# Weights that stay in SBUF and weights that are loaded ahead: the borders between three stages of a graph-network kernel

## The chip, the cores and the metric

The kernel runs on one core of a Trainium2 chip. The core has a matrix engine (PE, with its weight loads shown as PEld), a vector engine (DVE), an activation engine (ACT), a general engine (POOL) and a queue engine (SP) that only issues transfers. ACT and POOL issue transfers too. The metric is the device time of one execution in microseconds (us), median over runs.

## What is computed

Two layers work on 12500 nodes with 256 features each. The first is a weighted sum over 200000 edges followed by a dense layer. The second normalizes the rows, scores four experts for each node by graph attention over 131072 edges and a self-loop each, picks two of the four, and adds their gated outputs.

```python
z = layernorm(x)
x = x + (segment_sum(z[src] * edge_weight[:, None], dst) @ W.T + b)
y = layernorm(x)                                   # 12500 x 256; the experts' input
h = (y @ W_gat).reshape(M, HEADS, NUM_EXPERTS)     # 4 heads x 4 experts
e = leaky_relu((h * att_src).sum(-1)[src2] + (h * att_dst).sum(-1)[dst2], 0.2)
alpha = softmax of e over the edges of each dst2
scores = layernorm(segment_sum(h[src2] * alpha, dst2) + b_gat, ln_gamma, ln_beta).mean over heads
g = softmax over the two highest scores, 0 for the other two experts
x = x + sum over experts of g[:, e] * (gelu(y @ W1[e] + b1[e]) @ W2[e] + b2[e])
```

## The kernel before

Nodes are padded to 98 tiles of 128 rows and worked on in 25 groups of up to four tiles. The program has five stages.

**Head** (to about 150 us). The edge lists are loaded and turned, `x` is normalized and stored as `z_rows`, and the dense layer's `W` is loaded, turned on PE and stored to DRAM as `w_turned` (L246 to L253). A zeroed buffer is stored to `gat_starts` (L254).

**Edge stage** (150 to 2691 us). For each group of edges POOL gathers rows of `z_rows` (L544), PE sums them into windows (L558) and DVE adds the windows to `acc_x`, the sums of all nodes, which lie in SBUF (pool `wide`, 99 x 256 floats, 101 KB of each partition). Beside it the second layer's edges are sorted. The order of PE, DVE and ACT is written out by hand. The stage ends in a branch (L608) on a value, which every engine passes by itself. Its body reads and writes the edge lists and `acc_x` in case an edge group spans more nodes than a window.

**Node stage** (2691 to 2916 us; lines 651 to 773). It loads the turned weights `w_t` from `w_turned`, and `b_all`, `wg` and `att`, by five transfers on ACT's queue (L664 to L668). Then a loop runs over the 25 groups with a lag between its parts: load `x` and add `b_all` on POOL (L690, L701), turn `acc_x` on PE (L680, copied to SBUF by ACT, L681), multiply by `w_t` (L719), add (L721, DVE), normalize, turn back into `yt` (two buffers), store `yt` as `y_t` (L740), multiply by `wg` (L747), form the attention terms in `nds`, store them as `gat_nodes` (L759, ACT's queue) and scatter starts of segments into `gat_starts` (L761, POOL, 98 scatters indexed by `seg2`).

**Expert stage** (2916 to 4590 us; lines 778 to 996). First `starts` is loaded from `gat_starts` (L788), and DVE makes four scans over it and a reduction of `far` (L836 to L860); these temporaries lie in the pool `pre`, which is released after them. Then 100 steps run, one for each group and expert: `up` (L936, two halves, gelu by ACT at L942) and `down` (L960, added by DVE at L964, stored to `expert_rows` at L968). Each group first loads `yt5` from `y_t` (L930). PE's order is written out by hand. Beside it POOL gathers `gat_nodes` by edge (L803), 11 gathers per step and at most four steps ahead of the experts, and DVE runs the attention over blocks of 128 gathers (L874 to L893). The experts' weights `w_1` and `w_2` (16 KB of each partition, each), and the biases `b_in` and `b_2`, are loaded at L912 to L917, after `pre` is released. A short serial piece closes the attention (pool `tail`, L1000 to L1043).

**Mixing stage** (4590 us to the end). Gates are formed for ranges of tiles from rows gathered by POOL (L1076), and the experts' rows are loaded, weighted, summed and stored group by group (L1145 to L1162).

All buffers come from pools that are laid on one another like a stack, lowest address first. A pool waits, by default, when it lands on bytes of released pools: all of its tiles wait for every user of those pools. The transfers, DVE, ACT and POOL instructions outside hand-written regions are put in order by a planner that simulates the program: an engine takes, of what is ready, what stands first in the program. Once placed, an engine's queue is strictly in order.

In the expert stage the stack is, from the bottom: `order` (4 KB), `G` (98.4 KB), `starts` (20.5 KB), then `pre` (`far`, `keep2`, `scan` of 4 KB each, and small ones). After `pre` is released, `w_1`, `w_2`, `b_in` and `b_2` lie on its bytes, and above them `yt5` (two buffers of 4 KB), `fo` and `hh`.

## Time and profile before

| | us |
|---|---|
| median of three runs (lowest, highest) | 4203.77 (4192.69, 4206.19) |
| the profiled execution: its own time | 4920.08 |
| its span, first to last instruction | 4918.3 |
| busy in the span: PE, DVE, ACT, POOL | 3782.7, 2395.4, 1394.8, 2858.2 |

The profiled execution is 17% longer than the median of the runs without a profile; no view says where the extra lies. Times in views are microseconds from the start of the span. A timeline row has a start, a length (several instructions are merged when "x" is over 1), the engine ("SPq" is SP's queue issuing a transfer), the line, the operation, output and input, and in brackets the idle time before it with what ended it. A windows row has the stretch, its length, each engine's busy time with its count of instructions, the granted clock of PE (1.00 is full), the busy share of the 16 transfer engines, and what they moved in GB/s.

### The profile page before, as it was taken

How to read it: one execution, taken by the hardware profiler on the slowest of the kernel's cores; microseconds unless marked ns; L12 is line 12 of the kernel's file. 1: busy time of each engine (PE TensorE's matmuls, PEld its weight loads, DVE VectorE, ACT ScalarE, POOL GpSimd, SP SyncE). 2: the span in 40 equal slices, each digit the busy share in tenths (PEclk: the TensorE clock that was granted, in tenths of full speed). 3: DMA queues.
4: the chain of work that ended last, by engine and by line, in shares of the span. 5: the costliest groups of instructions: out<-in, count | busy, mean ns of one | idle time of the engine just before them, and what ended most of it. 6: DMA issues, size and time to landing. Idle time of an engine off the chain costs nothing. (4 is left out here: it accounts for less than half of the span.)

```text
span 4918.3 us, 54552 instructions
## 1 busy us (share of the span) xinstructions
PE 3782.7 (77%) x18969; PEld 2708.4 (55%) x18970; DVE 2395.4 (49%) x5474; ACT 1394.8 (28%) x3289; POOL 2858.2 (58%) x2825
## 2 busy tenths in 40 slices
PE   0556788878887878878888968889898988889445
PEld 0445566655665656656665855555555555555324
DVE  6555566666666666666665970211202202112267
ACT  4112344433333434333443211112112111112112
POOL 1567566655556556656665776666666666663430
PEclk6778899988998989999998978999999999999667
DMA  7232223322222223222222552222222222221488
GB/s 249 83 86 84 77 84 86 90 78 75 80 79 83 78 78 87 81 78 82 85 84 82 182 159 77 55 52 64 55 47 56 63 51 55 51 60 58 140 211 314
DMA packets 265845, 457.42 MB, mean 93 GB/s; under 512 B 67943, under 2 KB 168705, under 8 KB 264289
## 3 DMA queue, kind: packets, MB, share of 16 engines
q0 software_dynamic: 114128, 219.11, 18.4%
q1 hardware_dynamic: 111663, 207.52, 12.0%
q10 hardware_dynamic: 39778, 27.28, 1.7%
q8 instruction: 153, 2.51, 0.2%
q14 instruction: 123, 1.01, 0.1%
HBM read 334.05 MB, written 119.66 MB: 92 GB/s over the span
## 5 line engine op out<-in xcount | busy, mean ns | idle before, releaser
L544 POOL DMA_INDIRECT gt<-z_rows,src x1563 | 1564.1, 1001 | 1083.3 <-PE win L558 430.1
L803 POOL DMA_INDIRECT G<-gat_nodes,order x1024 | 1021.6, 998 | 549.3 <-issue 287.3
L960 PE MATMUL po<-w,hh 128*128 128x256 f32 x3136 | 749.6, 388 | 137.1 <-issue 92.9
L558 PE MATMUL win<-gt,oh_w 128*128 128x256 f32 x3126 | 811.2, 414 | 27.0 <-DMA gt<-z_rows,src 24.0
L936 PE MATMUL ph<-yt,w 128*128 128x512 f32 (+1 forms) x1600 | 756.1, 613 | 51.1 <-issue 45.2
L960 PEld LDWEIGHTS po<-w,hh 128*128 128x128 f32 x3136 | 607.0, 194 | 325.8 <-issue 194.2
L964 DVE TENSOR_TENSOR fo<-po,b 128x512 f32<-128x512 f32 x196 | 133.9, 689 | 1290.8 <-PE po L960 459.2
L484 DVE TENSOR_SCALAR st<-along,place_l,code 128x1024 bf16<-128x1024 f16 x1024 | 541.7, 570 | 437.6 <-PE place L453 107.4
L558 PEld LDWEIGHTS win<-gt,oh_w 128*128 128x128 f32 x3126 | 639.9, 210 | 128.7 <-issue 26.4
L942 ACT ACTIVATE hh<-ph,b 128x512 f32<-128x512 f32 (+1 forms) x400 | 248.5, 675 | 1255.6 <-PE ph L936 601.6
L550 ACT ACTIVATE oh_w<-hit_w,w 128x128 f32<-128x128 bf16 x1563 | 496.1, 391 | 379.7 <-DVE hit_w L334 165.1
L492 PE MATMUL perm<-st,to_p 128*128 128x512 bf16 x2048 | 568.2, 403 | 0.0
L936 PEld LDWEIGHTS ph<-yt,w 128*128 128x128 f32 x1600 | 319.8, 200 | 381.8 <-issue 364.1
L444 PE MATMUL look<-oh_lo,same_hi 128*128 128x128 bf16 x1024 | 236.1, 231 | 290.3 <-ACT next L456 151.9
L448 PE MATMUL look<-next,oht 98*128 98x128 f32 x2044 | 419.4, 314 | 0.0
L456 ACT ACTIVATE next<-place 98x256 f32<-98x256 f32 x511 | 193.4, 379 | 597.0 <-PE place L453 195.1
L448 PEld LDWEIGHTS look<-next,oht 98*128 98x128 f32 x2044 | 330.7, 204 | 35.9 <-issue 1.6
L463 DVE TENSOR_TENSOR sel<-look,oh_lo 128x512 f32<-128x512 f32 x256 | 175.6, 686 | 327.1 <-remote 119.2
L444 PEld LDWEIGHTS <-same_hi 128*128 128x128 bf16 x1024 | 104.0, 102 | 345.8 <-ACT next L456 191.8
L492 PEld LDWEIGHTS <-to_p 128*128 128x128 bf16 x2048 | 188.4, 102 | 137.9 <-issue 27.4
L436 ACT ACTIVATE same_hi<-bank 128x512 bf16<-128x512 f32 x256 | 152.4, 595 | 377.1 <-PE win L558 94.3
L565 DVE SCALAR_TENSOR_TENSOR acc_x<-win,in,acc_x 128x256 f32 x522 | 247.2, 474 | 19.6 <-PE win L558 15.6
(278 smaller groups left out, 3735.6 us busy)
## 6 DMA issues: line engine op xcount, KB each, us to landing
expert_rows<-fo SPq DMA_DIRECT2D x48, 1024.0 KB
fo_in<-expert_rows SPq DMA_DIRECT2D x24, 2048.0 KB
gt<-z_rows,src POOLq DMA_INDIRECT x1563
G<-gat_nodes,order POOLq DMA_INDIRECT x1024
xt<-in_x SPq DMA_DIRECT2D x24, 512.0 KB
z_rows<-xt ACTq DMA_DIRECT2D x24, 512.0 KB
x_two<-in_x SPq DMA_DIRECT2D x12, 1024.0 KB
x_rows<-x_two SPq DMA_DIRECT2D x12, 1024.0 KB
```

The lines of the kernel that those rows point to most:

```text
L444: first = nc.tensor.matmul(look[:, i % GT + k, :], b["m"][:, i + k, :], one(b["ol"], i + k), start=True, stop=False)
L448: nc.tensor.matmul(look[:, i % GT + k, :], b["oht"][:, i + k, :], nxt[:, k, :], start=False, stop=True)
L484: last = nc.vector.tensor_scalar(st[:, k, :], along, b["l"][:, i + k:i + k + 1], code2[:, c:c + 1], ALU.is_equal, ALU.mult)
L492: first = nc.tensor.matmul(perm[:, h, :], one(b["p"], i + k), st[:, k, h * 512:(h + 1) * 512], start=(c == 0), stop=(c == NC2 - 1), skip_g ...
L544: there = [nc.gpsimd.indirect_dma_start(out=rows[j], out_offset=None, in_=Z, in_offset=IND(ap=idx[:, c:c + 1], axis=0)) for j, c in enumer ...
L550: there += [nc.scalar.activation(hots[j], one(hit, j), AF.Copy, scale=w[:, c:c + 1]) for j, c in enumerate(chunks)]
L558: i = nc.tensor.matmul(win, h, r, start=(j == 0), stop=(j == len(rows) - 1))
L565: return nc.vector.scalar_tensor_tensor(to, win, m, to, ALU.mult, ALU.add)
L803: i = nc.gpsimd.indirect_dma_start(out=G[:, t + 1, :], out_offset=None, in_=NODE, in_offset=IND(ap=order[:, t:t + 1], axis=0))
L936: i = nc.tensor.matmul(ph[:, :n], w_1[:, e, k, f * P:(f + 1) * P], yts[g][:, :n, k, :], start=(k == 0), stop=(k == 1))
L942: i = nc.scalar.activation(item["hh"][:, f, :n * P], ph[:, :n].rearrange("p t m -> p (t m)"), AF.Gelu, bias=b_1[:, e * NF + f:e * NF + f + 1])
L960: m = nc.tensor.matmul(po[:, a, :], item["hh"][:, f, i * P:(i + 1) * P], w_2[:, e, f, :], start=(f == 0), stop=(f == NF - 1))
```

## The change

The turned `W` is no longer stored to DRAM and read back: ACT writes it to `w_t` in a new pool `ahead_of`, which is opened between `first_two` and `wide` and holds `w_t`, `b_all`, `wg` and `att` (3.3 KB) until the end of the node stage. The last three are loaded in the head. The experts' weights get a pool at the very bottom of the expert stage's stack, on the bytes of `first_two`, `ahead_of` and the lower part of `acc_x`, and their loads stand first in that stage's program. `order`, `G` and `starts` lie above them, and `pre` and the experts' `io` pool now begin at the same address, one after the other. All pools of the node and expert stages but `tail` get `reuse_waits="tile"`: each tile waits only for the users of earlier tiles on its own bytes (in PSUM, its own bank).

```diff
-    WT = nc.dram_tensor("w_turned", (D, D), F32).ap()
...
+    ahead_of = tc.alloc_tile_pool(name="ahead_of", bufs=1)
+    w_t = ahead_of.tile([P, 2, D], F32, name="w_t")
+    b_all = ahead_of.tile([P, D], F32, name="b_all")
+    wg = ahead_of.tile([P, 2, HC], F32, name="wg")
+    att = ahead_of.tile([P, 2, HC], F32, name="att")
     wide = tc.alloc_tile_pool(name="wide", bufs=1)
...
         w_in = late.tile([P, 2, D], F32, name="w_in")
         nc.sync.dma_start(w_in, W.rearrange("(c p) i -> p c i", p=P))
-        w_out = late.tile([P, 2, D], F32, name="w_out")
         for i in range(2):
...
-            nc.scalar.activation(w_out[:, i, :], pt[:, :2, :].rearrange("p o q -> p (o q)"), AF.Copy)
-        nc.sync.dma_start(WT.rearrange("(c p) o -> p c o", p=P), w_out)
+            nc.scalar.activation(w_t[:, i, :], pt[:, :2, :].rearrange("p o q -> p (o q)"), AF.Copy)
+        nc.scalar.dma_start(b_all, b[None, :].to_broadcast([P, D]))
+        nc.scalar.dma_start(wg, W_gat.rearrange("(c p) k -> p c k", p=P))
+        for k, a in enumerate((att_src, att_dst)):
+            nc.scalar.dma_start(att[:, k, :],
+                                a.rearrange("h c -> (h c)")[None, :].to_broadcast([P, HC]))
...
-        gp = s2.enter_context(tc.tile_pool(name="gp", bufs=3))
+        gp = s2.enter_context(tc.tile_pool(name="gp", bufs=3, reuse_waits="tile"))
...
+        fixed = s2.enter_context(tc.tile_pool(name="fixed", bufs=1, reuse_waits="tile"))
-        w_t = fixed.tile([P, 2, D], F32, name="w_t")
-        b_all = fixed.tile([P, D], F32, name="b_all")
-        wg = fixed.tile([P, 2, HC], F32, name="wg")
-        att = fixed.tile([P, 2, HC], F32, name="att")
...
-        nc.scalar.dma_start(w_t, WT.rearrange("(c p) o -> p c o", p=P))
-        nc.scalar.dma_start(b_all, b[None, :].to_broadcast([P, D]))
-        nc.scalar.dma_start(wg, W_gat.rearrange("(c p) k -> p c k", p=P))
-        for k, a in enumerate((att_src, att_dst)):
-            nc.scalar.dma_start(att[:, k, :],
-                                a.rearrange("h c -> (h c)")[None, :].to_broadcast([P, HC]))
...
     wide.release()
+    ahead_of.release()
     first_two.release()
     with ExitStack() as s3:
-        big = s3.enter_context(tc.tile_pool(name="big", bufs=1))
-        ps = s3.enter_context(tc.tile_pool(name="ps3", bufs=2, space=PSUM))
+        NF = FF // P
+        wp = s3.enter_context(tc.tile_pool(name="wp5", bufs=1, reuse_waits="tile"))
+        w_1 = wp.tile([P, C, 2, FF], F32, name="w_1")
+        w_2 = wp.tile([P, C, NF, D], F32, name="w_2")
+        b_in = wp.tile([C * NF, P], F32, name="b_in")
+        nc.sync.dma_start(b_in, b1.rearrange("e (f p) -> (e f) p", p=P))
+        for e in range(C):
+            nc.sync.dma_start(w_1[:, e], W1[e].rearrange("(k p) f -> p k f", p=P))
+            nc.sync.dma_start(w_2[:, e], W2[e].rearrange("(k p) d -> p k d", p=P))
+        b_2 = wp.tile([P, C, D], F32, name="b_2")
+        nc.sync.dma_start(b_2, b2[None, :, :].to_broadcast([P, C, D]))
+        big = s3.enter_context(tc.tile_pool(name="big", bufs=1, reuse_waits="tile"))
+        ps = s3.enter_context(tc.tile_pool(name="ps3", bufs=2, space=PSUM, reuse_waits="tile"))
...
-        pre = tc.alloc_tile_pool(name="pre", bufs=1)
+        pre = tc.alloc_tile_pool(name="pre", bufs=1, reuse_waits="tile")
...
         with ExitStack() as s5:
-            wp = s5.enter_context(tc.tile_pool(name="wp5", bufs=1))
-            io = s5.enter_context(tc.tile_pool(name="io", bufs=2))
...
-            w_1 = wp.tile([P, C, 2, FF], F32, name="w_1")
-            w_2 = wp.tile([P, C, NF, D], F32, name="w_2")
-            b_in = wp.tile([C * NF, P], F32, name="b_in")
-            nc.sync.dma_start(b_in, b1.rearrange("e (f p) -> (e f) p", p=P))
...
+            io = s5.enter_context(tc.tile_pool(name="io", bufs=2, reuse_waits="tile"))
+            hp = s5.enter_context(tc.tile_pool(name="hp", bufs=2, reuse_waits="tile"))
+            pe = s5.enter_context(tc.tile_pool(name="ps5", bufs=3, space=PSUM, reuse_waits="tile"))
             b_1 = wp.tile([P, C * NF], F32, name="b_1")
```

More of the change, by code (lines that the diff above doesn't have):

```diff
@@ L651, in gnn_gat_moe @@
     with ExitStack() as s2:
-        gp = s2.enter_context(tc.tile_pool(name="gp", bufs=3))
-        small = s2.enter_context(tc.tile_pool(name="small2", bufs=3))
-        ps = s2.enter_context(tc.tile_pool(name="ps2", bufs=2, space=PSUM))
+        gp = s2.enter_context(tc.tile_pool(name="gp", bufs=3, reuse_waits="tile"))
+        small = s2.enter_context(tc.tile_pool(name="small2", bufs=3, reuse_waits="tile"))
+        ps = s2.enter_context(tc.tile_pool(name="ps2", bufs=2, space=PSUM,
+                                              reuse_waits="tile"))
         flow = [{} for _ in range(NG)]
-        fixed = s2.enter_context(tc.tile_pool(name="fixed", bufs=1))
-        w_t = fixed.tile([P, 2, D], F32, name="w_t")
-        b_all = fixed.tile([P, D], F32, name="b_all")
-        wg = fixed.tile([P, 2, HC], F32, name="wg")
-        att = fixed.tile([P, 2, HC], F32, name="att")
+        fixed = s2.enter_context(tc.tile_pool(name="fixed", bufs=1, reuse_waits="tile"))
         ND = 6
@@ L902, in gnn_gat_moe @@
         with ExitStack() as s5:
-            wp = s5.enter_context(tc.tile_pool(name="wp5", bufs=1))
-            io = s5.enter_context(tc.tile_pool(name="io", bufs=2))
-            hp = s5.enter_context(tc.tile_pool(name="hp", bufs=2))
-            pe = s5.enter_context(tc.tile_pool(name="ps5", bufs=3, space=PSUM))
-            NF = FF // P
-            w_1 = wp.tile([P, C, 2, FF], F32, name="w_1")
-            w_2 = wp.tile([P, C, NF, D], F32, name="w_2")
-            b_in = wp.tile([C * NF, P], F32, name="b_in")
-            nc.sync.dma_start(b_in, b1.rearrange("e (f p) -> (e f) p", p=P))
-            for e in range(C):
-                nc.sync.dma_start(w_1[:, e], W1[e].rearrange("(k p) f -> p k f", p=P))
-                nc.sync.dma_start(w_2[:, e], W2[e].rearrange("(k p) d -> p k d", p=P))
-            b_2 = wp.tile([P, C, D], F32, name="b_2")
-            nc.sync.dma_start(b_2, b2[None, :, :].to_broadcast([P, C, D]))
+            io = s5.enter_context(tc.tile_pool(name="io", bufs=2, reuse_waits="tile"))
+            hp = s5.enter_context(tc.tile_pool(name="hp", bufs=2, reuse_waits="tile"))
+            pe = s5.enter_context(tc.tile_pool(name="ps5", bufs=3, space=PSUM, reuse_waits="tile"))
             b_1 = wp.tile([P, C * NF], F32, name="b_1")
```

## The prediction

> **What bounds the kernel now.** I read the page's slices first (PE is busy 8 to 9 tenths nearly everywhere), then windows by stage, then the queues' waits and the timelines at the two borders that the change touches. The chain of waits covers only the mixing stage and says nothing of these borders. Inside the expert stage PE sets the pace: 91.44 of the 100 us from 3200 are matmuls. Between the node stage and the experts PE has almost nothing:
>
> ```profile
> 2895.00:2900.00 5.00, 4.49 (x32) 3.58 (x31) 4.86 (x25) 1.84 (x5) 3.21 (x4) 0.94 1.11 229
> 2900.00:2905.00 5.00, 4.34 (x21) 3.94 (x20) 1.52 (x7) 0.60 (x1) 3.78 (x5) 0.50 0.74 191
> 2905.00:2910.00 5.00, 1.89 (x8) 1.78 (x8) 0.93 (x6) 0.60 (x1) 1.99 (x3) 0.50 0.22 61
> ...
> 2910.00:2958.00 48.00, 1.57 (x5) 0.60 (x5) 27.27 (x42) 0.00 (x0) 38.40 (x29) 0.50 0.32 100
> ...
> 3200.00:3300.00 100.00, 91.44 (x302) 58.58 (x301) 8.89 (x13) 15.06 (x24) 64.56 (x70) 0.97 0.23 54
> ```
>
> The reader is to see 48 us without matmuls of weight, and transfer engines that are full (share 1.11) until 2900. What ends the hole is in SP's waits and timeline:
>
> ```profile
> SPq L912 <- DVE starts L860: 34.8, 1, 34.8
> ...
> 2917.26 0.32 SPq L788 DMA_DIRECT2D starts<-gat_starts  x1
> 2917.69 0.84 SPq L930 DMA_DIRECT2D yt<-y_t  x2
> 2953.46 0.33 SPq L912 DMA_DIRECT2D b_in<-in_L_ffn_b  x1
> 2953.84 0.42 SPq L914 DMA_DIRECT2D w<-in_L_ffn_W  x1
> ...
> 2926.97 1.07 DVE L836 TENSOR_SCALAR keep<-starts 128x1024 f32<-128x1024 f32 x1 [8.79 <-DMA starts<-gat_starts]
> ...
> 2932.66 1.19 DVE L841 TENSOR_REDUCE spot<-far 128x1 f32<-128x1024 f32 x1
> ...
> 2944.24 9.08 DVE L860 TENSOR_TENSOR_SCAN starts<-keep,c,starts 128x1024 f32<-128x1024 f32 x4
> ...
> 2958.43 13.45 PE L936 MATMUL ph<-yt,w 128*128 128x512 f32 x24 [2.95 <-DMA w<-in_L_ffn_W]
> ```
>
> The weights lie on the bytes of `pre`, so SP holds them for 34.8 us, until DVE's last scan ends at 2953.3. `yt5` was asked for at 2917.69, being above them. The other border and the end of the experts:
>
> ```profile
> 2692.12 0.46 ACTq L664 DMA_DIRECT2D w_t<-w_turned  x1
> ...
> 2695.75 1.57 ACT L681 ACTIVATE agt<-pt 128x512 f32<-128x512 f32 x3 [11.02 <-issue]
> ...
> 2699.87 2.35 POOL L701 TENSOR_TENSOR x_two<-x_two,b_all 128x1024 f32<-128x1024 f32 x1 [28.40 <-DMA x_two<-in_x]
> ...
> 2702.25 0.69 DVE L721 TENSOR_TENSOR x_two<-x_two,po 128x512 f32<-128x512 f32 x1 [9.95 <-POOL x_two L701]
> ...
> 4590.68 0.36 SPq L968 DMA_DIRECT2D expert_rows<-fo  x1
> ...
> 4590.75 0.48 DVE L820 COPY as_rows<-pt 4x128 f32<-4x128 f32 x2
> ```
>
> **The change part by part.**
>
> *Head.* ACT gets four transfers more (0.59 + 0.56 + 0.83 + 0.50 = 2.48 us in the node stage's rows) and SP loses one (0.37). They come after ACT's copy that ends at 132.6; ACT's next instruction is at 150.0, after 17.40 us of waiting for DVE. That cover hides them; without it they cost 2.5. I take 0.
>
> *Border of edge and node stage.* Five issues leave ACT's queue (2692.12 to 2695.18), which held the copies of `agt` until 2695.75, and PE's wait of 3.67 us for `w_t` goes. But the next late thing is already there: DVE's first addition waits for POOL, and POOL for the 1 MB of `x_two`, asked for at 2692.14. The first `x_two` lies on the edge lists, which the branch's body uses, so its tile still waits until DVE has left the branch (2691.5): at most 0.6 us earlier. The `w_t`, `b_all` and small loads (about 0.4 MB) no longer share the engines; at the 263 GB/s of 2710 to 2720 that is 1.5 us. Bounds 0.6 to 3 us, taken 1.5. DVE is busy 194.91 of the stage's 220 us, so its start moves its end.
>
> *Where the experts' weights can start.* By sizes, the new stack is `w_1` (16 KB) on `first_two` (6 KB), `ahead_of` (3.3 KB) and the first 7 KB of `acc_x`; `w_2`, `b_in` and `b_2` on `acc_x` alone. `acc_x` is last read by turns at about 2891; `seg2`, in `first_two`, is read by the last scatter (2914.89), which is also what `starts` waits for. So `w_2`, `b_in` and `b_2` (2.6 MB) are asked for at about 2892, and `w_1` (2.1 MB) at 2917.3, ahead of `starts` since it stands first in the program.
>
> *Early part.* Issuing costs SP 0.33 + 4 x 0.47 + up to 2.60 = 4.8 us; SP's queue is free from 2892.34 (end of the issue at 2891.85) to 2897.03, so that is covered to within a fraction. The bytes are not: they stand before the store of the third last `yt`, issued at 2897.49, for whose buffer ACT waits 6.75 us (until 2907.41), and behind ACT the last `wg` products, `nds`, the last two scatters and `starts`. 2.6 MB at 330 GB/s (2965 to 2970, when weights were loading) are 8 us. If only that store releases ACT, the node stage ends 8 later; if something else does, 0. I take 5, above the middle because the share there is 1.11.
>
> Here a rule of the Trainium skill speaks against the change: "DMA: Bandwidth & Descriptors", "Issuing engines are not separate DMA queues", says that transfers from all issuers run on the same 16 engines and interleave. Its section on the anatomy of a transfer has a fit of 2.0 us plus bytes over 436 GB/s. By the fit `starts` (2.6 MB) takes 8.0 us; the trace has 9.7 (2917.26 to 2926.97). By the fit 2.1 MB ahead of it add 4.8 us; by the trace's 354 GB/s (2960 to 2965) 5.9. I use the trace; by the fit this part would be 1.1 us better and the early part (6.0 in place of 8) about 1.2, so the sum some 2 us better.
>
> *The new wait.* `pre` and `io` now begin at the same address. The first `yt5` buffer lies on `far`, the second on `keep2`. So the load of the first group's `yt5`, which cost nothing before, waits on SP for L841 on DVE, and the second's for L860. What stands behind them on SP is stores of `fo`, not needed until a step is done; who waits for the first is PE. The time: scatters end 2917.3 + 5 = 2922.3; `starts` arrives 9.7 + 5.9 later, 2937.9; L841 ends 6.9 after that (2926.97 to 2933.85 in the rows), 2944.8; `yt5` of 0.5 MB takes about 4 (the first `w_1` took 2953.84 to 2958.43), 2948.8. Against 2958.43 that is 9.6 us earlier. Gelu needs `b_1`, copied by DVE at L921; with `b_in` there by 2900 I expect the planner to put it into DVE's wait for `starts`.
>
> *Expert stage.* PE's 100 steps follow its start. POOL begins 5 us later and PE 9.6 earlier. POOL needs 44 gathers until 2985 + 5 and then 11 x 1.25 = 13.75 us a step; 128 for the first attention block are there at 2990 + 8 x 13.75 = 3100. That block began at 3115.1 and would now begin at 3105. Covered, by 5 us; if not, DVE holds PE's additions for the difference.
>
> *Tail.* `tail` still waits by pool. It lay on the weights, whose last user is PE; it now lies on `io`, whose last user is the store issued at 4590.68. DVE's first copy at 4590.75 therefore waits for 0.5 MB to land: 0.4 + about 3.6 (as above, an estimate) = 4 us; bounds 0 and 5. Behind it lie the gather of `row`, the gathers L1076 and the first gates, which is the chain of waits. `bg` to `nodes` (2.4 us of SP) may go earlier, but the gates, not SP, release the mixing.
>
> *Sum:* -1.5 - 9.6 + 4 = -7 us: 4913 for the profiled execution (4920.08). These are waits of fixed length, so I carry them to the median of plain runs unscaled: 4203.77 - 7 = 4197. 0.3% is 12.6 us, about what a measurement of this kernel can tell from no change.
>
> **The rivals.**
>
> *A, as summed:* chance 0.50; 4188 to 4203.
>
> *B, the queue is kinder:* `starts` goes ahead of `w_1` and the early bytes do not delay the node stage. Then L841 ends at 2933.9, PE starts at 2938, 20.4 earlier; with -1.5 and +4 it is -18: 4186. If also `yt5` didn't land on `far`, PE would start when `w_1` lands, 2922, and the time would be 4170. For it: both loads wait for the same scatter, so a tie decides. Against: ties go to the program's order. 0.26.
>
> *C, slower:* all 4.7 MB stand ahead of `starts`, and `b_1` stays behind the four scans of L860 in DVE's queue. `starts` is late by 14, with the node stage's 8 by 22; the scans end at 2975 and the first gelu follows at 2977, where it was at 2966.4. PE has only four banks for `ph`, so it stands: +11, with the tail +4 and the border -1.5 it is +13: 4217. It turns to a loss once `starts` is late by more than 11.6. For it: L921 stands behind L860 in the program. Against: DVE waits 8.79 us for `starts`. 0.15.
>
> *D, nothing there:* the planner's order makes the loads wait as before, or PE is held by something else at the same time; the tail's +4 and -1.5 remain: 4206. 0.09.
>
> **How the numbers follow.** Faster by over 0.3%: B and the lower edge of A, 0.28. Slower by over 0.3%: most of C and what a changed order of DVE in the expert stage may cost, 0.17. Within: 0.55. The range takes in B's main case and C's lighter ones: 4180 to 4216.
>
> **What would show it.** PE's first L936 at about 2947 (2937 by B, over 2958 by C); SP's wait of L930 on DVE L841 in place of L912 on L860; L788 issued after four L914; DVE L836 starting near 2936; ACT's wait for the last `yt` longer than 6.75; no idle time at L719 for `w_t`, but L721 still waiting for POOL; L820 4 us behind the last L964. I am wrong if PE starts before 2930, if `tail` starts at once, or if the steps themselves take another time.

## The result, and the profile after

| | us |
|---|---|
| before, median of 10 runs beside the changed kernel | 4201.92 (4192.69 to 4206.19) |
| after, median of 10 runs | 4215.93 (4209.60 to 4224.52) |
| ratio, with its 95% interval | 1.0035 (1.0027 to 1.0043) |
| the profiled execution after: its own time, its span | 4211.29, 4209.5 |

The changed kernel is slower by 14.0 us (11.3 to 18.1); a gain of 7 had been forecast. Chips differ: the kernel before takes 4200 to 4203 us on three of them ("the 4200 pace" below) and 4916 to 4919 us on two ("the 4900 pace"), where PE's mean granted clock is lower (0.87 to 0.88 instead of 0.94), and the profile on which the prediction rests, at 4920.08 us, has the second pace. So the trace after is set beside a second trace of the kernel before (run `e12_before_same_chip` below, span 4204.5), and every ratio to before is between runs on one chip.

**The hole between node stage and experts.** One window of the changed kernel (columns as in the prediction's first fence):

```profile
2455.00:2502.00 47.00, 0.75 (x2) 0.16 (x2) 15.94 (x27) 1.28 (x1) 37.53 (x33) 0.50 0.55 175
```

The hole is as long as it was. More is transferred in it (share 0.55, where 48 us of before had 0.32), and PE still has nothing. SP's waits and timeline, then DVE and PE, say why:

```profile
SPq L929 <- DVE spot L853: 21.5, 1, 21.5
SPq L929 <- DVE starts L871: 19.1, 1, 19.1
...
SPq L786 <- DMA gat_starts<-nds,seg: 10.1, 2, 8.9
...
2449.70 0.40 SPq L784 DMA_DIRECT2D b_in<-in_L_ffn_b  x1
2460.57 0.38 SPq L786 DMA_DIRECT2D w<-in_L_ffn_W  x1
2461.00 2.20 SPq L787 DMA_DIRECT2D w<-in_L_ffn_W  x1
...
2470.14 0.55 SPq L799 DMA_DIRECT2D starts<-gat_starts  x1
...
2492.69 19.78 SPq L929 DMA_DIRECT2D yt<-y_t  x2
```

```profile
2460.77 0.17 DVE L920 COPY b<-ph 128x16 f32<-128x16 f32 x1
...
2485.83 1.07 DVE L847 TENSOR_SCALAR keep<-starts 128x1024 f32<-128x1024 f32 x1 [24.89 <-DMA starts<-gat_starts]
...
2491.47 1.19 DVE L852 TENSOR_REDUCE spot<-far 128x1 f32<-128x1024 f32 x1
...
2503.04 9.08 DVE L871 TENSOR_TENSOR_SCAN starts<-keep,c,starts 128x1024 f32<-128x1024 f32 x4
...
2501.34 0.37 PE L829 MATMUL pt<-ident,v 128*4 128x128 f32 x1 [12.76 <-DVE fix_i L862]
...
2502.90 12.09 PE L935 MATMUL ph<-yt,w 128*128 128x512 f32 x24
```

SP waits at L786, the first `w_1`, for the last scatter. `w_2` stands behind it, since the loop alternates the two, and all nine transfers (four of `w_1`, four of `w_2`, and `b_2`; 4.7 MB) go ahead of `starts`, which is asked for 11.0 us after the last scatter's end (2459.1) and lands 15.7 us later. The predicted wait of `yt5` for `far` is there (L929 behind DVE's `spot`). But PE does not start right behind that load: in its queue the transposes of the scans' carries (L829) stand ahead of the first L935.

**The border of edge and node stage.** DVE's first addition came 10.9 us after the cast of `order`, its last instruction of the edge stage (L603; L611 in the changed kernel), in the second trace of before, and 8.3 us in the changed kernel (2239.72 to 2247.97). It waits for POOL, as it did:

```profile
2245.60 4.65 POOL L699 TENSOR_TENSOR x_two<-x_two,b_all 128x1024 f32<-128x1024 f32 x2 [14.75 <-DMA x_two<-in_x]
...
2247.97 1.29 DVE L719 TENSOR_TENSOR x_two<-x_two,po 128x512 f32<-128x512 f32 x2 [7.76 <-POOL x_two L699]
```

**The tail.** First the second trace of before, then the changed kernel, from the last addition of the experts on (timelines of DVE, POOL and SP):

```profile
3925.81 0.69 DVE L964 TENSOR_TENSOR fo<-po,b 128x512 f32<-128x512 f32 x1 [5.68 <-PE po L960]
3926.60 0.48 DVE L820 COPY as_rows<-pt 4x128 f32<-4x128 f32 x2
...
3930.38 0.16 DVE L1007 TENSOR_TENSOR m_row<-m,row 128x4 f32<-128x4 f32 x1 [1.59 <-DMA row<-gat_run,fix_i]
...
3927.24 1.04 POOL L1036 DMA_INDIRECT row<-gat_run,fix_i  x1 [96.69 <-DVE carried L827]
...
3937.33 0.97 POOL L1076 DMA_INDIRECT R<-gat_run,end  x1 [2.02 <-DMA gat_run<-fixed,fix_i]
...
3938.18 0.81 SPq L1062 DMA_DIRECT2D nodes<-gat_nodes  x1
```

```profile
3919.67 0.69 DVE L963 TENSOR_TENSOR fo<-po,b 128x512 f32<-128x512 f32 x1 [5.69 <-PE po L959]
3923.31 0.48 DVE L831 COPY as_rows<-pt 4x128 f32<-4x128 f32 x2 [2.94 <-DMA expert_rows<-fo]
...
3934.45 0.16 DVE L1006 TENSOR_TENSOR m_row<-m,row 128x4 f32<-128x4 f32 x1 [8.84 <-DMA row<-gat_run,fix_i]
...
3924.14 0.94 POOL L1035 DMA_INDIRECT row<-gat_run,fix_i  x1 [99.81 <-DMA bg<-in_L_ffn_b_gat]
...
3941.40 0.96 POOL L1075 DMA_INDIRECT R<-gat_run,end  x1 [2.01 <-DMA gat_run<-fixed,fix_i]
...
3922.73 0.81 SPq L1061 DMA_DIRECT2D nodes<-gat_nodes  x1
```

From the last addition to the first gather of `R`, which opens the mixing, it is 11.5 us before and 21.7 us after. DVE's copy waits 2.94 us for the store of `fo`. Then the gather of `row` takes 10.3 us from its start until DVE uses it (3924.14 to 3934.45), where it took 3.1 before (3927.24 to 3930.38): `nodes` (98 x 24 floats in 128 partitions, 1.2 MB in pieces of 96 bytes) is now asked for 1.4 us ahead of it. Before, `nodes` waited for the whole tail.

The stretches in one table, worked out from the timelines (us, from start to start; each column is one profiled execution at the 4200 pace; the experiments are told below):

| stretch | before, e12 | after | e4 | e5 | e6 | e7 | e15 |
|---|---|---|---|---|---|---|---|
| cast of `order` to first addition | 10.9 | 8.3 | 8.0 | 7.9 | 8.0 | 8.1 | 8.8 |
| first addition to first gather of `G` | 213.0 | 211.4 | 214.0 | 208.9 | 213.9 | 215.5 | 218.3 |
| last `wg` product to first `up` | 49.8 | 52.1 | 49.3 | 48.0 | 35.1 | 9.6 | 50.9 |
| first gather to last addition of the experts | 1458.3 | 1460.3 | 1457.9 | 1459.1 | 1456.7 | 1457.8 | 1458.9 |
| from there to first gather of `R` | 11.5 | 21.7 | 15.8 | 13.9 | 15.6 | 16.3 | 11.5 |
| from there to the end | 267.2 | 268.1 | 266.7 | 268.8 | 267.9 | 267.1 | 268.3 |
| ratio of times to before | 1.0001 | 1.0035 | 1.0013 | 1.0013 | 1.0016 | 1.0019 | 1.0014 |

From the cast on, after against before: -2.6 - 1.6 + 2.0 + 10.2 + 0.9 = +8.9 us (the third row overlaps its neighbours and is not in the sum). The edge stage ends at 2239.7 after and 2243.6 before, but in the traces whose edge stage has the same code it ends anywhere from 2237.1 to 2246.2, so a single trace says nothing there. Nor can this pair hold all of the 14.0 us: its two executions took 4211.29 and 4206.27 us, 5.0 apart, the one 4.6 under its kernel's median and the other 3.3 over that of the runs beside it.

### The profile page after: what moved, and what is told of

It reads as the page before. It is cut to its first block, busy times and chain, and to the rows that moved or that the text cites. A ratio compares the mean times of both kernels' runs of the same rounds, so it can differ in the third digit from the quotient of the medians.

```text
span 4209.5 us, 54518 instructions
## 1 busy us (share of the span) xinstructions
PE 3542.2 (84%) x18969; PEld 2600.8 (62%) x18970; DVE 2390.4 (57%) x5474; ACT 1421.5 (34%) x3289; POOL 2902.5 (69%) x2825
## 3 DMA queue, kind: packets, MB, share of 16 engines
q0 software_dynamic: 114128, 219.11, 21.3%
q1 hardware_dynamic: 111391, 207.26, 13.9%
## 5 line engine op out<-in xcount | busy, mean ns | idle before, releaser
L552 POOL DMA_INDIRECT gt<-z_rows,src x1563 | 1603.5, 1026 | 603.3 <-issue 403.0
L566 PE MATMUL win<-gt,oh_w 128*128 128x256 f32 x3126 | 767.4, 397 | 200.2 <-DMA gt<-z_rows,src 150.4
L566 PEld LDWEIGHTS win<-gt,oh_w 128*128 128x128 f32 x3126 | 596.3, 197 | 316.9 <-issue 192.9
L959 PE MATMUL po<-w,hh 128*128 128x256 f32 x3136 | 721.2, 384 | 51.0 <-ACT hh L941 36.4
L959 PEld LDWEIGHTS po<-w,hh 128*128 128x128 f32 x3136 | 603.1, 193 | 219.8 <-issue 87.5
L935 PE MATMUL ph<-yt,w 128*128 128x512 f32 (+1 forms) x1600 | 706.6, 585 | 0.0
L941 ACT ACTIVATE hh<-ph,b 128x512 f32<-128x512 f32 (+1 forms) x400 | 249.5, 676 | 1046.8 <-PE ph L935 1044.4
L500 PE MATMUL perm<-st,to_p 128*128 128x512 bf16 x2048 | 524.1, 378 | 0.0
L935 PEld LDWEIGHTS ph<-yt,w 128*128 128x128 f32 x1600 | 304.6, 190 | 288.9 <-issue 277.5
L456 PE MATMUL look<-next,oht 98*128 98x128 f32 x2044 | 393.8, 300 | 0.0
L456 PEld LDWEIGHTS look<-next,oht 98*128 98x128 f32 x2044 | 309.5, 192 | 37.6
L342 DVE TENSOR_TENSOR oh_hi<-twice,hi 128x784 bf16<-128x784 bf16 x256 | 143.4, 560 | 96.8 <-PE place L366 96.7
```

Of the source, the lines that this page charges most:

```text
L456: nc.tensor.matmul(look[:, i % GT + k, :], b["oht"][:, i + k, :], nxt[:, k, :], start=False, stop=True)
L500: first = nc.tensor.matmul(perm[:, h, :], one(b["p"], i + k), st[:, k, h * 512:(h + 1) * 512], start=(c == 0), stop=(c == NC2 - 1), skip_g ...
L552: there = [nc.gpsimd.indirect_dma_start(out=rows[j], out_offset=None, in_=Z, in_offset=IND(ap=idx[:, c:c + 1], axis=0)) for j, c in enumer ...
L566: i = nc.tensor.matmul(win, h, r, start=(j == 0), stop=(j == len(rows) - 1))
L935: i = nc.tensor.matmul(ph[:, :n], w_1[:, e, k, f * P:(f + 1) * P], yts[g][:, :n, k, :], start=(k == 0), stop=(k == 1))
L941: i = nc.scalar.activation(item["hh"][:, f, :n * P], ph[:, :n].rearrange("p t m -> p (t m)"), AF.Gelu, bias=b_1[:, e * NF + f:e * NF + f + 1])
```

## The experiments

**The kernel before again.** Unchanged code, three times.

> The kernel before, unchanged, for a profile of an execution as long as the runs without one, so that its stages can be set beside those of the changed kernel (span 4209.5). Time: 4203, ratio 1.000. If the loss is made at the border of node stage and experts alone, the stretch from the last `wg` product to the first L936 is about 12 us shorter here than the 52 us of the changed kernel; if it is made in the experts' steps, the stretch is equal and the experts last some 12 us less here than the 1412 us (2502.9 to 3914.6) of the changed one.

> The kernel before, unchanged, once more for a profile on a chip where it takes 4200 us, to set its stages beside those of the changed kernel (first addition of the node stage to last `wg` product 202.8 us; last `wg` to first L935 52.1; first to last gather 1364.0; last gather to last L935 91.2; start of the last addition of experts to `fixed` 18.3; from there to the end 271). Theory 'POOL and the first attention block pace the experts': the pause before the experts is 48.5 us here, 3.6 shorter, but the stretch from first to last gather and the 91 us behind it are the same within 3 us, so the border's 3.6 us are not in the result; the tail is 10 us shorter. What is left of the 14 us must then stand in the node stage or ahead of it. Rival: the gathers' stretch is shorter here, and the loss is made in the experts' steps.

> The kernel before, unchanged, for a trace of an execution of about 4200 us. In five traces of changed kernels at that length the stretches are: first addition of the node stage to first gather 209 to 215 us, first gather to last addition of the experts 1457 to 1460 us, start of that addition to `fixed` 18.3 us (8 with `tail` by tile). With `tail` by tile the changed kernel still measured 1.0013 [1.0007, 1.002] of before, 5.5 us. If the tile waits or the new stack lengthen the node stage, this trace has it 5 us or more shorter (about 205); if they lengthen the experts, their stretch is 5 us or more shorter here (about 1452); if both agree within 2 us, the rest stands ahead of the node stage, in the head or the edge stage.

The first two ran at the 4900 pace: 1.0028 (1.0005 to 1.0052) and 0.9995 (0.9966 to 1.0024). The first is the same kernel and its interval still leaves out 1, so at that pace a ratio tells nothing under half a per cent, and only local stretches are used of those traces. The third gave the column above: the node stage is no shorter in it than after (213.0 against 211.4), the experts' stretch agrees within 2.0 us, the tail is 10.2 shorter. So in this pair neither the tile waits nor the new stack lengthened the two stages; what is left is the tail, and some 5 of the 14 us that no stretch of the pair holds.

**Which wait holds the start of the experts** (e1, then e3; 4900 pace).

```diff
         b_in = wp.tile([C * NF, P], F32, name="b_in")
-        nc.sync.dma_start(b_in, b1.rearrange("e (f p) -> (e f) p", p=P))
-        for e in range(C):
-            nc.sync.dma_start(w_1[:, e], W1[e].rearrange("(k p) f -> p k f", p=P))
-            nc.sync.dma_start(w_2[:, e], W2[e].rearrange("(k p) d -> p k d", p=P))
         b_2 = wp.tile([P, C, D], F32, name="b_2")
-        nc.sync.dma_start(b_2, b2[None, :, :].to_broadcast([P, C, D]))
...
         nc.sync.dma_start(starts, STARTS[:E2, :].rearrange("(p l) c -> p l c", l=L2))
+        nc.sync.dma_start(b_in, b1.rearrange("e (f p) -> (e f) p", p=P))
+        for e in range(C):
+            nc.sync.dma_start(w_1[:, e], W1[e].rearrange("(k p) f -> p k f", p=P))
+            nc.sync.dma_start(w_2[:, e], W2[e].rearrange("(k p) d -> p k d", p=P))
+        nc.sync.dma_start(b_2, b2[None, :, :].to_broadcast([P, C, D]))
```

```diff
         pre = tc.alloc_tile_pool(name="pre", bufs=1, reuse_waits="tile")
+        pad = pre.tile([P, 2 * L2], F32, name="pad")
         far = pre.tile([P, L2], F32, name="far")
```

> The changed kernel with one thing moved: the loads of the experts' weights stand behind the load of `starts` in the program, not ahead of it. In the changed kernel `starts` was asked for at 2470.14, 11.0 us after the last scatter's end at 2459.1, and DVE's scans could begin at 2485.83. Theory 'queue order' (nine loads in front of `starts` hold it back): `starts` is asked for within 1 us of the last scatter and DVE's L847 begins about 10 to 10.5 us after it, so 16 us earlier; PE's first L935 comes 10 to 16 us earlier, and the time is about 4201. Rival 'new stack' (the loss comes from `yt5` on `far` or from the experts' steps): the time stays within 4 us of 4216.

> The changed kernel with 8 KB of unused bytes laid first in `pre`, so that the two `yt5` buffers lie on no temporary of `pre`; the first load of `yt5` then waits for nothing on DVE. In the changed kernel it was asked for at 2492.69 and PE's first L935 came at 2502.90. Prediction's step (PE waits for this load, and for nothing else): PE starts about 10 us or more earlier, time 4205. Rival 'PE's own queue': two transposes of the scans' carries (L829, L841) stand in PE's queue ahead of the first L935, and they wait for DVE's scans, which end at 2502.5; then PE starts at the same time, the gain is under 1 us and the time 4215.

In e1 `starts` is asked for 8.1 us after the last `wg` product, and the hole is 35.2 us, where it is 48.0 to 52.1 in the six traces with the weights ahead of `starts`: the order in SP's queue was worth 13 to 17 us of PE's start. The ratio was 1.0050 (1.0021 to 1.0078), no gain. In e3 the hole is 49.6 us; the ratio 1.0056 (1.0029 to 1.0084). Its `yt5` was asked for at 2935.53, and PE's timeline shows what it waited for:

```profile
2965.41 0.37 PE L830 MATMUL pt<-ident,v 128*4 128x128 f32 x1 [12.83 <-DVE fix_i L863]
2966.60 0.27 PE L842 MATMUL pt<-ident,carried 4*128 4x4 f32 x1 [0.82 <-DVE carried L840]
2966.80 0.37 PE L830 MATMUL pt<-ident,low 128*4 128x128 f32 x1
2966.96 3.62 PE L936 MATMUL ph<-yt,w 128*128 128x512 f32 x4
```

The experts begin at once behind the transposes. PE's own queue ties them to the scans, 17 us after `starts` has landed; `yt5` on `far` costs nothing.

**The tail** (e4, then e5; 4200 pace).

```diff
-        tail = s3.enter_context(tc.tile_pool(name="tail", bufs=1))
+        tail = s3.enter_context(tc.tile_pool(name="tail", bufs=1, reuse_waits="tile"))
```

```diff
         one = s4.enter_context(tc.tile_pool(name="one", bufs=1))
+        pad = one.tile([P, 12 * 1024], F32, name="pad")
```

> The changed kernel with `tail` too waiting by tile. In the kernel before, the stretch from the start of the last L964 to the copy into `fixed` by the last addition of the tail (L1041) is 8.0 us; in the changed kernel it is 18.3 us: 2.9 us of it before DVE's first copy (the wait for the last store of `fo`), and 10.3 instead of 3.1 us for the gather of `row` (L1035), which was issued 1.4 us behind the load of `nodes`. Theory 'tail': without the wait DVE's copy follows at once, the gather of `row` is issued ahead of `nodes`, and the stretch comes back to 8 to 10 us; 8 to 10 us less in the time. Prediction's step (only the landing costs): 3 to 4 us less, since `nodes` is under way anyway. Rival 'elsewhere': the stretch shrinks, and the time does not, since another thing (load of `nodes`, `fo_in`) then holds the mixing stage.

> The changed kernel with 48 KB of unused bytes laid first in pool `one`, so that `one` lands on `G` as well and its loads (`bg` to `nodes`) wait for the end of the tail's work on `G`, as before the change; `tail` still waits by pool for the last store of `fo`. Theory 'nodes in front of row': the gather of `row` takes 3 us again and not 10.3, the first copy still waits 2.9 us, and the tail's stretch is 11 us instead of 18.3; 7 us less in the time. Rival: the gather is slow for another reason (behind the store of `fo`), and the stretch stays at 17 to 18 us.

Both measured 1.0013 (e4 1.0007 to 1.0020, e5 1.0006 to 1.0020), by the ratios some 9 us better than the changed kernel. In e5, with `nodes` held back, the gather of `row` takes 2.4 us (3920.22 to 3922.63), the first copy still waits 2.78, and the tail is 13.9 us: `nodes` was some 7 of the 10.2 us. In e4 the gather slips past `nodes`, but the scatter of `fixed` behind it does not:

```profile
3925.55 1.01 POOL L1042 DMA_INDIRECT gat_run<-fixed,fix_i  x1 [10.04 <-DVE fixed L1040]
3934.81 0.96 POOL L1075 DMA_INDIRECT R<-gat_run,end  x1 [8.25 <-DMA gat_run<-fixed,fix_i]
```

POOL waits 8.25 us for the scatter where it waited 2.02 before. The stretch that the expectation named came back to 6.1 us, but the wait moved to the scatter: to the first gather of `R` e4 gave back 5.9 of the 10.2 us.

**Both repairs, and an early start** (e6, e7; 4200 pace). e6 is e1 with e4's tail. In e7, which has e4's tail too, `w_2` lies on the bytes that the scatters read and `w_1` on `acc_x` alone; the first `yt5` has a place of its own; `far`, `keep2` and `scan` lie in rows of `G`; and the scans with their transposes are a function that is called behind step 3.

```diff
-        w_1 = wp.tile([P, C, 2, FF], F32, name="w_1")
         w_2 = wp.tile([P, C, NF, D], F32, name="w_2")
+        w_1 = wp.tile([P, C, 2, FF], F32, name="w_1")
...
+        yt_0 = wp.tile([P, GT, 2, P], F32, name="yt_0")
+        nc.sync.dma_start(yt_0, YT[:, :GT])
         for e in range(C):
             nc.sync.dma_start(w_1[:, e], W1[e].rearrange("(k p) f -> p k f", p=P))
-            nc.sync.dma_start(w_2[:, e], W2[e].rearrange("(k p) d -> p k d", p=P))
...
         nc.sync.dma_start(starts, STARTS[:E2, :].rearrange("(p l) c -> p l c", l=L2))
+        for e in range(C):
+            nc.sync.dma_start(w_2[:, e], W2[e].rearrange("(k p) d -> p k d", p=P))
...
+        def spare(row):
+            return G[:, row:row + 43, :].rearrange("p l c -> p (l c)")[:, :L2]
...
+        far = spare(800)
...
+                    if step == 3:
+                        scans()
```

> The changed kernel with both repairs: the experts' weights loaded behind `starts`, and `tail` waiting by tile. The stretch from the last `wg` product to the first L935 was 35 us with `starts` first (52 in the changed kernel, 48.5 before). If the two terms add: 17 + 9 us less than the changed kernel, 13 + 3 (start of the node stage) = about 16 less than before where the rest is equal: ratio about 0.996 to before. Rival 'the clock takes it back': the stretches shrink as said, and the first 200 us of the experts get a lower granted clock than after the longer pause (0.89 against 0.92 in the run with `starts` first), so that the time is that of before.

> A version drawn from the readings: `w_2` and not `w_1` lies on the bytes that the scatters still read; `w_1` and the first `yt5` (in a place of its own) are asked for right behind the node stage's last store, then `starts`, then `w_2`; the temporaries of `pre` lie in rows of `G` that are gathered last, so that nothing of the experts lies on them; and the scans' transposes stand in PE's queue behind step 3 and not ahead of the first L935; `tail` waits by tile. If PE's queue and the weights are what holds the experts, PE's first L935 (here L944) comes within 10 us of the last `wg` product, 40 us earlier than in both kernels, and the time is up to 45 us less than before (ratio 0.990). Rival 'POOL is next': POOL's gathers start no earlier and need 13.75 us for 11, a step of PE about 14; PE is held by DVE's attention blocks and gets back 20 us or less.

Ratios 1.0016 (1.0006 to 1.0026) and 1.0019 (1.0012 to 1.0026). PE started 35.1 and 9.6 us after the last `wg` product instead of 52.1, and neither is faster than e4. The row of the table that doesn't move says why: from first gather to last addition it is 1457 to 1460 us in all of them. DVE's waits, of the changed kernel, e6 and e7:

```profile
DVE G L885 <- DMA G<-gat_nodes,order: 128.8, 9, 21.9
```

```profile
DVE G L885 <- DMA G<-gat_nodes,order: 138.9, 9, 24.5
```

```profile
DVE G L893 <- DMA G<-gat_nodes,order: 164.4, 9, 45.7
```

In DVE's queue the first attention block stands behind 16 additions of the experts, eight steps, and needs 128 gathers. They are there 172 to 174 us after the first gather, whenever PE began (2640.1 - 2467.5 before; 2633.5 - 2459.4 after; 171.5 in e7). The additions behind the block wait with it, PE has two banks for `po`, and every later block ties the two again. When PE begins earlier, DVE only comes to the first block earlier and waits longer there: 45.7 us in e7.

PE feels most of this through ACT. ACT's queue is in order too, and the block's exponentials (L894, L896) stand in it ahead of gelus (L941). The second block in the changed kernel:

```profile
2801.74 0.69 DVE L885 TENSOR_TENSOR G<-G,starts 128x512 f32<-128x512 f32 x1 [13.98 <-DMA G<-gat_nodes,order]
...
2807.02 0.63 ACT L894 ACTIVATE starts<-starts 128x512 f32<-128x512 f32 x1 [13.90 <-DVE starts L893]
...
2808.95 1.27 ACT L941 ACTIVATE hh<-ph,b 128x512 f32<-128x512 f32 x2
...
2810.27 5.23 PE L959 MATMUL po<-w,hh 128*128 128x256 f32 x16 [6.04 <-ACT hh L941]
```

Over all of the experts' steps PE waits 36.4 us for ACT and 14.4 us for DVE.

**Is it DVE's order, or POOL's gathers themselves?** First a test of the gathers, at the 4900 pace.

```diff
             for t in range(turn * PER_TURN, min((turn + 1) * PER_TURN, L2)):
+                if t % 16 == 15:
+                    continue
```

> The changed kernel with every 16th of the 1024 gathers of edges left out (their places in `G` are zeroed once by DVE), so the attention of those edges is not computed. Theory 'POOL paces the experts' (a gather takes 0.95 us and 0.30 to the next): 64 gathers less are 64 x 1.33 = 85 us off POOL's 1364; the experts end earlier until PE's own pace holds them (100 steps of about 13.5 us, so at most some 50 us earlier); time 30 to 50 us less than 4216. Theory 'PE paces the experts' (prediction): within 5 us of the changed kernel.

0.9872 of before (0.9833 to 0.9911), 4869.01 against 4919.43: nearer to "POOL paces". But PE's granted clock between 2990 and 4480 us was 0.95, where it is 0.93 in e3, as well, and at this pace POOL sat 247.4 us waiting for the experts' additions. I take it as inconclusive. The order itself:

```diff
-            nc.vector.tensor_add(e, e, d)
+            i = nc.vector.tensor_add(e, e, d)
+            tc.add_manual_dep(i.ins, turned[-1].ins.name, mybir.DependencyInfo(
+                mybir.DependencyClass.Sync, mybir.DependencyReason.DATA),
+                reason="not ahead of its step")
...
-                    if under_way and next(under_way, under_way) is under_way:
-                        under_way = None
+                    for _ in range(1 if step < 90 else 2):
+                        if under_way and next(under_way, under_way) is under_way:
+                            under_way = None
```

This was put on e6 (e10, e13), on e7 (e11, e14), on the kernel before (e16) and on the changed kernel (e17). The first block then stands behind 28 additions (the added dependency keeps a block from going ahead of its step), and in the last ten steps two pieces of a block are taken for one.

> The version with `starts` first and `tail` by tile, and the attention blocks kept from DVE's queue until the step behind which they stand in the program (the first block behind 28 additions of the experts, where it stood behind 16), and two pieces of a block for each of the last ten steps. Theory 'DVE waits in order': in the version without this, DVE sat 139 us in nine waits for gathers with the experts' additions queued behind it, and three versions whose PE began at 2471, 2487 and 2503 all ended the experts 1461 to 1464 us after the first gather. With the blocks later DVE's wait for gathers goes to under 20 us, PE keeps its own pace, and its earlier start counts: experts 20 to 45 us shorter, ratio to before 0.990 to 0.997. Rival 'PE paces': no difference to the version without it (1.0016).

> The version with the experts' early start (first L944 9.6 us behind the last `wg` product) with the same order of the attention blocks. If DVE's wait was what took the early start back, this one is faster than the one before by the 16 us by which PE begins earlier: ratio to before 0.986 to 0.994. If POOL's gathers are the bound whatever DVE does, both are within 5 us of each other.

> The version with `starts` first, `tail` by tile and the attention blocks kept in the program's order, again, where the kernel before takes about 4200 us. It measured 0.9966 [0.9945, 0.9986] where before took 4919 us, while without the order of blocks the same stretch of experts lasted as long whether PE began at 2471, 2487 or 2503. Theory 'DVE waits in order for gathers': DVE's nine waits (139 us) go, PE keeps its own pace (100 steps of 13.5 to 13.8 us), experts 30 to 45 us shorter, ratio 0.990 to 0.994. Rival 'POOL's gathers are the bound whatever DVE does': the last gather comes at the same time, the ratio stays at 1.0016.

> The version with the experts' early start and the blocks in order, again, where before takes about 4200 us (0.9960 [0.993, 0.9989] where it took 4919). By 'DVE waits in order' PE's earlier start by 16 us counts in full: ratio 0.986 to 0.991. By 'POOL is the bound' no faster than the run before this one.

> The kernel before with only the order of the attention blocks changed (the first behind 28 additions of the experts instead of 16, two pieces of a block for each of the last ten steps). In the version with `starts` first and `tail` by tile this took the experts from 1457 to 1381 us behind the first gather where before takes 4200 us (ratio 0.9832). Theory 'DVE waits in order for gathers' holds for the kernel before as well: its nine waits (129 us) go and, as its PE begins 16 us later than in that version, ratio 0.985 to 0.989. Rival 'the new stack is needed': less than half of it.

> The changed kernel as it is (weights ahead of `starts`, `tail` by pool) with the same order of the attention blocks. With DVE no longer waiting for gathers PE's start counts: it comes 52 us behind the last `wg` product, 2 to 3 us later than in the kernel before, and the tail is 10 us longer, so about 12 us more than the kernel before with this order (ratio to it 1.003); against the version with both repairs (0.9832) the 17 us of a later PE and the 10 us of the tail: 0.989 to 0.992 of before. Rival 'the border never counts': only the tail's 10 us more than that version, 0.9855.

At the 4900 pace 0.9966 (0.9945 to 0.9986) for e10 and 0.9960 (0.9930 to 0.9989) for e11: less than the half per cent that a ratio can tell at that pace, and no difference between the two. At the 4200 pace:

| | e16: before | e17: after | e13: both repairs | e14: early start |
|---|---|---|---|---|
| ratio to before | 0.9843 (0.9830 to 0.9857) | 0.9871 (0.9856 to 0.9887) | 0.9832 (0.9819 to 0.9844) | 0.9795 (0.9782 to 0.9808) |
| last `wg` to first `up`, us | 49.1 | 49.3 | 35.6 | 11.3 |
| first `up` to last addition | 1354.1 | 1353.4 | 1352.5 | 1362.4 |
| first gather to last addition | 1394.1 | 1396.0 | 1380.8 | 1365.4 |
| last gather to last addition | 58.1 | 58.1 | 36.4 | 21.3 |
| last addition to first gather of `R` | 11.5 | 21.9 | 15.8 | 16.4 |

DVE's waits for gathers are gone (8.2 us in e14, none in the others), and PE's longest wait within the steps is 2.9 us (e14; 0.8 in the others). The windows of the experts' whole stretch, of before (e12) and of e16:

```profile
2507.90:3925.80 1417.90, 1367.57 (x4737) 908.92 (x4737) 267.38 (x465) 291.62 (x443) 991.95 (x1001) 0.98 0.24 65
```

```profile
2499.56:3853.60 1354.04, 1353.20 (x4737) 902.41 (x4737) 268.41 (x465) 283.60 (x437) 992.13 (x1001) 1.00 0.25 68
```

So it was DVE's order: it cost the kernel before and the changed one alike some 64 us, and it hid every shift of the border. With it gone PE's start counts: the experts end 15 us earlier behind the first gather in e13 than in e17, and 15 more in e14. There two bounds nearly meet: PE is busy for 1355.9 of the 1362.4 us, and the 1024 gathers take 1344 us, with the last addition only 21 us behind the last one. e17 against e16 is 1.0032 (4147.95 over 4134.54), 13.4 us, 10.4 of them in the tail; the border is equal (49.1 and 49.3 us), where I had expected 2 to 3 us. The gain of e13 over e16 was smaller than the 16 us expected: 0.0011, about 5 us, and the two intervals overlap. In the traces 13.3 us are won from first gather to last addition and 2.9 ahead of the first addition; 4.2 are lost in the tail, 2.2 in the mixing and 6.9 in a longer node stage (219.8 against 212.9 us). e14, at 4113.94 us, is some 2% faster than both kernels.

**The head's part alone** (e2 at the 4900 pace, e15 at the 4200 pace): `ahead_of` and its four loads, all else as before.

> The kernel before with the head's part of the change alone: turned W written to `w_t` in `ahead_of`, `b_all`, `wg` and `att` loaded in the head, everything after it as before (pools wait by pool, experts' weights loaded late). Prediction's step: -1.5 us, so 4202 and no difference that can be measured. Rival: the first product of the node stage waits for ACT and SP less than the trace of before let see, up to 5 us gained; or the four loads in the head delay the head's ACT and the edge stage starts later, up to 3 us lost.

> The head's part alone, again, where before takes about 4200 us. Its start of the node stage was 2 us earlier than before's in the traces at 4900 us (8.7 instead of 10.7 and 11.2 us from the cast of `order` to the first addition). If nothing else of the head's part matters: ratio 0.9995. If the 5.5 us that are left with `tail` by tile come from the head or the edge stage (`acc_x` and the edge lists lie 3.3 KB higher): ratio 1.001 to 1.002.

1.0004 (0.9973 to 1.0036) and then 1.0014 (1.0008 to 1.0021): at the 4200 pace it costs 5.9 us (3.4 to 8.8), not 0. The trace has the node stage begin 2.1 us earlier and last 5.3 longer. In the traces the loss lies in a stretch of 15 us that begins 23 us after the cast of `order`; the windows of before (e12) and of e15:

```profile
2266.57:2281.57 15.00, 12.82 (x72) 11.33 (x72) 14.24 (x50) 2.58 (x7) 10.21 (x8) 0.89 0.58 183
```

```profile
2265.43:2280.43 15.00, 12.78 (x59) 11.21 (x59) 12.13 (x39) 2.80 (x6) 8.58 (x6) 0.74 0.53 171
```

In e15 PE's clock falls to 0.50 for some 10 us after a gap of 2.2 us, PE is late, and DVE gets 2.1 us less done. In the changed kernel's trace the same stretch has a clock of 1.00. Of the nine traces at the 4200 pace that have the head's part, four show the dip (0.73 or 0.74; e7, e13, e14, e15), with node stages of 215.5 to 219.8 us, and five don't, with 208.9 to 214.6; the two of before's head and node stage have 0.89 and 213 us. What decides between the two is open. If most executions of the changed kernel had the dip and the profiled one had not, that could be the missing 5 us; this is argued, not shown. Weakly against it: e4 and e5 have the head's part too and measured 5.5 us over before, of which their traces show 4.3 and 2.4 us in the tail, so that 1 to 3 us are left for it.

## Why the prediction was wrong, step by step

Two steps of the sum failed: the new wait, put at -9.6 us, gave nothing, and the tail, put at +4, was 10.2.

*PE's 100 steps follow its start:* this step failed, so that the border's -9.6 us would not have counted even if PE had begun earlier: in e7 it begins 9.6 us after the last `wg` product instead of 52.1, and the experts end only 2.5 us sooner after the first gather. The step was read from "91.44 of the 100 us are matmuls" in a trace at the 4900 pace. Waits of that trace, then of the second trace of before:

```profile
POOL G L803 <- DVE fo L964: 249.0, 55, 11.4
DVE G L874 <- DMA G<-gat_nodes,order: 67.7, 9, 10.6
```

```profile
DVE G L874 <- DMA G<-gat_nodes,order: 129.2, 9, 21.0
POOL G L803 <- DVE fo L964: 30.5, 15, 9.1
```

In the first POOL mostly waits for the experts' additions; at the 4200 pace it is DVE that waits for POOL's gathers. The nine waits of DVE stood in the first trace too, 67.7 us of them, and of these blocks the prediction looked at the first alone: "Covered, by 5 us; if not, DVE holds PE's additions for the difference". The "if not" held.

*Head, 0:* not confirmed. The part alone measured +5.9 us (e15), with its gain at the next border already in it; how much of it is in the changed kernel is open.

*Border of edge and node stage, -1.5 (bounds 0.6 to 3):* right in kind, -2.6 in the pair of traces.

*Where the weights can start, early part +5:* wrong. Only `b_in` went early; `w_2` stood behind `w_1` in SP's queue. I had let `w_2` overtake, against the order of the loop.

*Starts +5.9 late:* its landing took 15.7 instead of 9.6 us, which is the price, but by chance: 4.7 MB stood ahead and not 2.1, and it was asked for 11.0 us after the last scatter, which was not priced. The fit that the prediction sets beside it stands in the Trainium skill ("DMA: Bandwidth & Descriptors", "Anatomy of one DMA — SWDGE (gpsimd) path") for transfers that GpSimd issues, and `starts` goes by SP's queue; the sum rests on the trace, which has 9.7 us.

*New wait on `far`, PE 9.6 us earlier:* the wait is there and decides nothing (e3). Forgotten were the transposes at the head of PE's queue. PE started 2.2 us later in the pair: 48.0 to 52.1 us after the last `wg` product over six traces with the weights ahead of `starts`, against 48.4 to 49.8 in four of the kernel before. So nothing was won of the 9.6.

*Tail, +4 (bounds 0 and 5):* the term that was mis-sized: 10.2 us. The landing was 2.9 of the 4 priced. The other 7 are the loads of `one`: "`bg` to `nodes` (2.4 us of SP) may go earlier, but the gates, not SP, release the mixing". They do go earlier, since `one` now lies on weights that only PE reads, and the small transfers on the gates' path queue behind them. The same page of the Trainium skill that was weighed for `starts` ("DMA: Bandwidth & Descriptors", "Issuing engines are not separate DMA queues": transfers of all issuers share the engines) spoke against this edit too; I applied it at one border only.

*Rivals:* C forecast 4217, and its first half is what the trace shows (4.7 MB ahead of `starts`). Its loss is not: `b_1` was copied early (L920), and the border cost nothing. That its time came close is chance. Of the 14.0 us, 8.9 are placed in the pair of traces; about 5 are not, and their cause stays open.

## What to carry to other kernels

Before a shift at a border is priced, find what ties the next stage to other engines: a block in an in-order queue that needs data at its own time absorbs every shift, and the stretch that stays equal while PE's start moves by 40 us points to it. When a profile's own time is far from the median, what paces in it need not be what paces in the runs: look whether the producer waits for the consumer or the consumer for the producer. When buffers move, list what is released as well as what is held; a bulk load that goes earlier lands in front of small transfers on the critical path.

## What the hardware showed that was not expected

A pause of PE costs more than its length. In the changed kernel's experts PE waits 50.8 us (36.4 for ACT, 14.4 for DVE), yet the stretch is 63 us longer than in e16 (1416.8 against 1354.1): the busy time is up from 1353.2 to 1365.6 us, at a clock of 0.98 instead of 1.00. The longest wait, 13.9 us, ends at 3152; a window around its end shows the clock at 0.50:

```profile
PE po L959 <- ACT hh L941: 36.4, 7, 13.9
PE po L959 <- DVE fo L963: 14.4, 2, 7.3
...
3141.00:3158.00 17.00, 6.02 (x14) 4.86 (x15) 12.65 (x22) 8.93 (x10) 10.61 (x11) 0.50 0.25 69
```

The five waits of 6.0 to 13.9 us all go with such a stretch, of 6.8 to 17.1 us; those of 1.1 and 2.1 us do not, and in e16, where the longest within the steps is 0.8, there is none. The Trainium skill ("TensorE: Matmul & The Clock Gate", "What's actually happening") has the clock halve after an idle window of about 3.4 us, which these waits agree with; the dip of e15 in the node stage came after a gap of only 2.2 us.

POOL's gathers take 0.95 us, but up to 2.6 us while DVE's scans run (after, 2493.86 to 2512.9). Between the scans of L867 and those of L871, which begin at 2503.04, a gather is fast again:

```profile
2502.16 1.08 POOL L814 DMA_INDIRECT G<-gat_nodes,order  x1 [0.30 <-issue]
2503.55 2.60 POOL L814 DMA_INDIRECT G<-gat_nodes,order  x1 [0.30 <-issue]
```

The skill ("SBUF — State Buffer", "SBUF: two separate sides") has DVE and GpSimd share a port pair that a DVE operation with two SBUF inputs holds alone against a GpSimd operation that reads SBUF; the rows agree in kind, and no run took the scans away to test it.
